# Cross-attention on one core: exponentials taken with tokens in partitions, values applied in 32x32 pieces of the array

## The chip, the cores and the metric

The kernel runs on one core of a Trainium2 chip. A core has TensorE (PE; its weight loads are shown apart as PEld), VectorE (DVE), ScalarE (ACT), GpSimd (POOL) and SyncE (SP, which issues most DMAs). The metric is device time in microseconds of one launch, as the median of several runs. Lower is better.

## The reference

One transformer block on `x` of 2 x 1024 tokens, 256 wide, with a context of 2 x 77 tokens. There are 16 heads of 16. All is float32.

```python
# layer norms inside have no gain or shift
q = (layernorm(x) @ Wq + bq); k = (ctx @ Wk + bk); v = (ctx @ Wv + bv)   # split in 16 heads of 16
att = q k^T / 4 ; att = att * mask - 1e10 * (1 - mask)
x = x + softmax(att) v @ Wo + bo
t = layernorm(x)
z = t + relu(t @ w1[0] + b1[0]) @ w2[0] + b2[0]                           # 256 -> 1024 -> 256; one expert counts
out = x + layernorm(z) * gamma + beta
```

## The kernel before

The 2048 tokens are cut into eight "halves" (`h` 0 to 7) of 256 tokens, each of them two tiles (`n` 0 and 1) of 128 tokens. Halves 0 to 3 use the first context, 4 to 7 the second.

A half goes through these steps, each a small function:

- `a_stats`, `a_norm`, `a_turn`: layer norm of `x` and four PE transposes. `a_hi` (ACT) rounds the turned input to fp32r, `a_lo` (DVE) keeps the rest, and `a_query` (L397) multiplies by `Wq` in three fp32r products: high by high, low by high, high by low. `Wq` was split in the same way at the start (`split_hi`, `split_lo`). `q_bias` (ACT) adds the bias.
- `s_scores` (L417): for each tile 8 float32 matmuls, four at a time in row strips of 32 (two heads share a strip; `kb` holds the keys with the other head's rows zeroed). Tokens lie in partitions, 16 heads x 77 keys in the free dimension.
- `s_mask` (L429, DVE) multiplies by the mask while it moves the scores from PSUM to `u` in SBUF; `s_bias` (L438, POOL) adds the large negative number; `s_max` and `s_max_act` (L443, L448, DVE) take the maximum of each head. The maximum is subtracted by DVE for 8 heads (`s_sub`, L453) and by ACT, head by head, for the other 8 (`s_sub_act`, L459).
- `s_turn` (L468): PE transposes each head, 128 tokens x 77 keys, into PSUM. `s_exp` (L473, ACT) takes the exponential of four heads at a time on the way to `pT`, which has keys in partitions.
- `s_out` (L481): values by numerators. The stationary operand is `vb`, 77 keys x 32 columns for a head (16 values and 16 ones, so that the sum of the exponentials comes out as well); 256 tokens stream. Four heads work at a time in column strips of 32.
- `s_norm` (L493 to L498, DVE): the result is turned in 32x32 blocks, and divided by the sums. `o_turn` (L511) turns back, `o_hi` and `o_lo` split, and `o_proj` (L529) multiplies by `Wo` in three fp32r products.
- `y_stats` to `y_lo`: the residual, second layer norm, transposes and split.
- FFN: `f_up` (L571) and `f_down` (L600) in three fp32r products each, with `f_relu`, `f_hi` (ACT) and `f_lo` (L589, POOL) between them; 4 steps `q` of 256 hidden units each.
- `z_stats` to `z_out`: the last layer norm and the store.

Which engine does what next is written out ahead of time: `Stages.order` takes every stage with an engine, a cost, its predecessors, the buffers (`rings`) that it needs and a rank (from `START`, `LATER`, `TILE_LAG`), and lays them one after the other; the program is then emitted in that order, and each engine keeps it. `ps` are seven PSUM banks that stages take and give back; an eighth holds small statistics. `u` has three buffers, `pT` two. 40 warm-up matmuls on zeros (`WARM`, 512 columns, L210) have the last rank and fill PE's gaps at the start.

`Wq` and `Wk` are loaded from ACT's queue, everything else from SP's, in the order of the `fetch` calls.

## Time and profile before

| | |
|---|---|
| Runs | 212.58, 211.70, 211.59 us; median 211.7 us |
| Profiled execution | 211.81 us; span from first to last instruction 210.0 us; mean granted PE clock 0.992 |
| Instructions | 1852 matmuls and 1852 weight loads on PE, DVE 336, ACT 386, POOL 151 |
| Costliest on POOL | L438 44.1 us, L589 40.9 us |
| Costliest on ACT | L473 34.2 us, L459 33.7 us, L580 26.6 us |
| Costliest on DVE | L443 and L448 25.3 us together, L429 24.1 us, L453 12.6 us, L493 11.4 us |
| DMA | 8.73 MB, of which 0.23 MB are PE's instructions |

A busy time counts the stretches in which at least one instruction of the group is under way. Matmuls are pipelined, so a mean duration is longer than the distance from one to the next. In a line of a group the last part is the time for which the engine stood idle just before, and who released it. A float32 product appears as two matmul records and two loads.

### The profile page before, as it was taken

The numbers are of one execution on the slowest core, as the hardware profiler recorded it, in microseconds if no ns is written. First come the engines' busy times: TensorE is split into PE (matmuls) and PEld (weight loads), VectorE is DVE, ScalarE is ACT, GpSimd is POOL, SyncE is SP. The second block draws the span as 40 slices with busy tenths as digits, with TensorE's granted clock in tenths as the row PEclk, the third lists the DMA queues.
The fourth block names the chain that finished last, engine by engine and source line by source line (L and its number), as shares of the span: only waits on it lengthen the run. The fifth ranks groups of instructions, "written<-read, shape, count | busy, mean of one in ns | idle before, by whom it ended". The sixth has DMA issues, their size and how long they took to land. (4 is left out here: it accounts for less than half of the span.)

```text
span 210.0 us, 4829 instructions
## 1 busy us (share of the span) xinstructions
PE 201.2 (96%) x1852; PEld 175.9 (84%) x1852; DVE 154.8 (74%) x336; ACT 155.3 (74%) x386; POOL 149.1 (71%) x151
## 2 busy tenths in 40 slices
PE   6999769999999999999999999999999999999995
PEld 1778556987996999799999778999988979999981
DVE  1678996999767992769999768999487667267234
ACT  3289998899894699993789997259997857624910
POOL 3469999899999967869998180197976573653741
PEclk9999997999999999999999999999999999999999
DMA  5997000000000000010000100001010000101011
GB/s 194 356 396 262 0 3 3 2 0 3 0 0 3 3 2 0 3 50 3 2 0 3 50 5 0 3 0 50 3 50 3 0 0 5 50 0 52 3 50 52
DMA packets 4807, 8.73 MB, mean 42 GB/s; under 512 B 662, under 2 KB 995, under 8 KB 4784
## 3 DMA queue, kind: packets, MB, share of 16 engines
q1 hardware_dynamic: 4496, 7.90, 10.3%
q10 hardware_dynamic: 288, 0.52, 0.7%
q8 instruction: 14, 0.23, 0.5%
q14 instruction: 9, 0.07, 0.1%
HBM read 6.33 MB, written 2.10 MB: 40 GB/s over the span
## 5 line engine op out<-in xcount | busy, mean ns | idle before, releaser
L438 POOL TENSOR_TENSOR u<-u,mb 128x616 f32<-128x616 f32 x32 | 44.1, 1399 | 9.5 <-DVE u L429 9.1
L589 POOL TENSOR_TENSOR hl<-h,hh 128x512 fp32r<-128x512 f32 x32 | 40.9, 1289 | 10.2 <-ACT hh L585 8.7
L571 PE MATMUL ps<-yh,w1h 128*128 128x256 f32 x128 | 37.4, 292 | 0.0
L473 ACT ACTIVATE pT<-ps 77x512 f32<-77x512 f32 x64 | 34.2, 593 | 3.9 <-PE ps L468 3.9
L600 PE MATMUL ps<-w2h,hh 128*128 128x256 f32 x128 | 37.0, 289 | 0.0
L468 PE MATMUL ps<-ident,u 128*77 128x128 f32 x256 | 34.9, 281 | 2.1 <-DVE u L453 1.3
L571 PE MATMUL ps<-yl,w1h 128*128 128x256 f32 x128 | 36.3, 283 | 0.0
L571 PE MATMUL ps<-yh,w1l 128*128 128x256 f32 x128 | 36.1, 282 | 0.0
L600 PE MATMUL ps<-w2h,hl 128*128 128x256 f32 x128 | 35.8, 279 | 0.0
L600 PE MATMUL ps<-w2l,hh 128*128 128x256 f32 x128 | 35.8, 279 | 0.0
L468 PEld LDWEIGHTS ps<-ident,u 128*77 128x77 f32 x256 | 29.5, 150 | 6.6 <-DVE u L453 2.2
L459 ACT ACTIVATE u<-u,mx 128x77 f32<-128x77 f32 x128 | 33.7, 357 | 0.6 <-DVE mx L448 0.6
L580 ACT ACTIVATE h<-ps,cols 128x256 f32<-128x256 f32 x64 | 26.6, 471 | 7.9 <-DVE ot L493 3.8
L571 PEld LDWEIGHTS ps<-yh,w1h 128*128 128x128 f32 x128 | 24.4, 191 | 1.7 <-issue 0.9
L429 DVE TENSOR_TENSOR u<-ps,mk 128x616 f32<-128x616 f32 x32 | 24.1, 792 | 2.0 <-PE ps L417 2.0
L600 PEld LDWEIGHTS ps<-w2h,hh 128*128 128x128 f32 x128 | 24.3, 190 | 1.2 <-issue 1.1
L571 PEld LDWEIGHTS ps<-yl,w1h 128*128 128x128 f32 x128 | 24.5, 191 | 0.2 <-DVE yl L554 0.2
L571 PEld LDWEIGHTS ps<-yh,w1l 128*128 128x128 f32 x128 | 24.5, 191 | 0.0
L600 PEld LDWEIGHTS ps<-w2l,hh 128*128 128x128 f32 x128 | 24.1, 188 | 0.0
L600 PEld LDWEIGHTS ps<-w2h,hl 128*128 128x128 f32 x128 | 24.1, 188 | 0.0
L585 ACT ACTIVATE hh<-h 128x512 fp32r<-128x512 f32 x32 | 20.0, 634 | 5.1 <-PE ps L600 4.5
L481 PE MATMUL ps<-pT,vb 77*32 77x256 f32 x256 | 16.8, 388 | 0.1
(96 smaller groups left out, 427.2 us busy)
## 6 DMA issues: line engine op xcount, KB each, us to landing
x<-in_x SPq DMA_DIRECT2D x8, 256.0 KB, 5.5
out<-tg SPq DMA_DIRECT2D x7, 256.0 KB, 2.0
wst<-in_L_ffn_w SPq DMA_DIRECT2D x4, 256.0 KB, 5.4
wst<-in_w SPq DMA_DIRECT2D x4, 256.0 KB, 6.0
rows<-in_rows SPq DMA_DIRECT2D x1, 512.0 KB
mk<-in_mask SPq DMA_DIRECT2D x1, 308.0 KB, 4.9
wq<-in_wq ACTq DMA_DIRECT2D x1, 256.0 KB
wk<-in_wk ACTq DMA_DIRECT2D x1, 256.0 KB, 4.6
```

The lines of the kernel that those rows point to most:

```text
L429: nc.vector.tensor_tensor(us[h, n][:, 8 * s : 8 * s + 8].rearrange("p (b h) t -> p b h t", b=2), ps[:, b0 : b0 + 2, :W].rearrange("p b (h ...
L438: nc.gpsimd.tensor_tensor(v, v, mb[:, h % HPB, n].unsqueeze(1).to_broadcast([P, 8, T]), ALU.add)
L459: nc.scalar.activation(u, u, AF.Identity, bias=mx[:, k : k + 1])
L468: nc.tensor.transpose(pt[:T, j], us[h, n][:, k], ident)
L473: nc.scalar.activation(pTs[h][:, i, :, n], pss.pop(("t", h, n, i))[:T], AF.Exp)
L481: nc.tensor.matmul(pos[h, s][r, e], lhsT=vb[:, h // HPB, k], rhs=pTs[h][:, 2 * s + e, j].rearrange("k n t -> k (n t)"), start=True, stop=True,
L571: nc.tensor.matmul(pz[:, i], lhsT=w[:, c, j * P : (j + 1) * P], rhs=v[:, c], start=(k == 0), stop=(k == 5))
L580: nc.scalar.activation(t[:, i], pz[:, i], AF.Relu, bias=b1[:, 2 * q + i : 2 * q + i + 1])
L585: nc.scalar.activation(hh[h, q], hs[h, q], AF.Copy)
L589: nc.gpsimd.tensor_tensor(hl[h, q], hs.pop((h, q)), f(hh[h, q]), ALU.subtract)
L600: nc.tensor.matmul(pys[h, ns[0]][:, n], lhsT=v[h, q][:, i, n * P : (n + 1) * P], rhs=w[:, j], start=(q == 0 and n == ns[0] and i == 0 and ...
```

## The change

Attention:

- The maximum (`s_max`) is taken by DVE for 8 heads at a time. `s_exp` is now ACT on `u` in place: one instruction for each head, `exp(u - max)` with the maximum as bias, 128 tokens in partitions and 77 keys. `s_sub`, `s_sub_act` and the PE transposes are gone.
- `s_turn` is now DVE: `u` is turned in square blocks of 32x32. One instruction turns keys 0 to 63 of all heads, a second the last 16 keys, two heads to a block. A block holds 32 keys in partitions and 32 tokens; the four row strips hold four different groups of 32 tokens.
- `s_out` works on 32x32 pieces of the array: row strip `r` holds one group of tokens and writes its own PSUM bank, column strip `j` one head. For a half it is 4 groups of heads x 3 pieces of keys (0 to 31, 32 to 63, the last 16) x 4 x 4 = 192 float32 calls of 64 columns. It takes four banks at once. `vb` holds the values in all four row strips and three pieces (`v_proj`, `v_copy`, `v_ones`, `ctz`); the value bias goes through `Wo` into `bo` once (`o_rows`, `o_bias`).
- `s_norm` turns with two instructions instead of one.
- The query and output projections are plain float32: four calls for a half each instead of 12 fp32r ones. `a_lo`, `o_hi`, `o_lo` and the splits of `Wq` and `Wo` go.

Beside it: all loads are on SP's queue, with small vectors packed behind the mask; some small copies go from DVE to ACT; 200 warm-up matmuls of 256 columns instead of 40 of 512; in the last half two `f_lo` are on DVE, the residual enters the FFN's sum by a matmul with the identity (`f_first`), and the centring (`z_center`) is done beside POOL's power. Costs, ranks and lags of the order are new throughout.

```diff
-WARM = 40
+WARM = 200
...
-GAP = 0.44
-TILE_LAG = 11.6
+GAP = 0.3
+TILE_LAG = 36.1
...
     def a_query(h):
...
             for d in range(2):
-                for w, v in ((wqh, xh[h]), (wqh, xl[h]), (wql, xh[h])):
-                    nc.tensor.matmul(
-                        pq[:, c], lhsT=w[:, d, c * P : (c + 1) * P], rhs=v[:, d], start=(k == 0), stop=(k == 5)
-                    )
-                    k += 1
+                nc.tensor.matmul(
+                    pq[:, c], lhsT=wq[:, d, c * P : (c + 1) * P], rhs=xh[h][:, d], start=(d == 0), stop=(d == 1)
+                )
...
-    def s_turn(h, n, i):
-        pt = pss["t", h, n, i] = bank(("tr", h, n, i), (P, 4, P))
-        for j, k in enumerate(heads(i)):
-            nc.tensor.transpose(pt[:T, j], us[h, n][:, k], ident)
...
+    def s_max(h, n, s):
+        mx = mxs[h, n, s] = work([P, 8], "mx", f"mx{h}_{n}{s}", 12)
+        nc.vector.tensor_reduce(mx, us[h, n][:, 8 * s : 8 * s + 8], AX.X, ALU.max, negate=True)
+
+    def s_exp(h, n, s, i):
+        mx = mxs[h, n, s] if i == 0 else mxs.pop((h, n, s))
+        for k in range(4 * i, 4 * i + 4):
+            u = us[h, n][:, 8 * s + k]
+            nc.scalar.activation(u, u, AF.Exp, bias=mx[:, k : k + 1])
+
+    def s_turn(h, n):
+        if n == 0:
+            pTs[h] = work([P, 40, 2, 32], "pT", f"pT{h}", RINGS["pT"])
+        u = us.pop((h, n))
+        nc.vector.transpose(pTs[h][:, :32, n], u[:, :, :64])
+        nc.vector.transpose(pTs[h][:, 32:, n], u[:, :, T - 16 :])
+
+    def s_out(h):
+        pos[h] = got = st.all["po", h]["slots"]["ps"]
+        for g in range(4):
+            s, e = g // 2, g % 2
+            for k in range(3):
+                for r in range(4):
+                    for j in range(4):
+                        i = 8 * s + 2 * j + e
+                        v = slice(32 * r, 32 * r + 32)
+                        o = ps[32 * j : 32 * j + 32, got[r], 128 * s : 128 * s + 128]
+                        nc.tensor.matmul(
+                            o.rearrange("p (n e t) -> p n e t", n=2, e=2)[:, :, e],
+                            lhsT=vb[v, h // HPB, k, i],
+                            rhs=pTs[h][v, 2 * i + k if k < 2 else 32 + i // 2],
+                            start=(k == 0), stop=(k == 2), skip_group_check=True,
+                            tile_position=(32 * r, 32 * j),
+                        )
...
     def s_norm(h, s):
+        t = work([P, 2, 4, 2, 32], "ot", f"ot{h}_{s}", 1)
+        for z in range(2):
+            b0 = pos[h][2 * z]
+            nc.vector.transpose(
+                t[:, :, 2 * z : 2 * z + 2].rearrange("p n r e d -> p n r (e d)"),
+                ps[:, b0 : b0 + 2, 128 * s : 128 * s + 128].rearrange("p r (n c) -> p n r c", n=2),
+            )
...
+    def f_first(h, n):
+        pys[h, n] = bank(("dt", h, n), (P, 2, E))
+        nc.tensor.matmul(pys[h, n][:, n], lhsT=ident, rhs=tg[h][:, n], start=True, stop=False, skip_group_check=True)
...
-    fetch("wqd", 0.9, lambda: None, ring=stage_ring("hh", "wqh", "wql"))
...
+    fetch_x(0, 1.3)
+    fetch("cd", 0.45, load, c_sb, a["c"])
+    fetch("wkd", 0.75, load_matrix, "wk", "wk", "hl", ring=stage_ring("hl", "pk"))
+    fetch("mkd", 0.9, load, mkc, a["mask"])
+    fetch("wqd", 0.7, load, wq, a["wq"])
+    fetch_x(1)
```

## The prediction

> **What bounds the kernel now.** I read the busy shares first, then the table by stage, then the groups of instructions, then PE's timeline. The chain that ended last covers the final 4 us only and says nothing of the middle.

> ```profile
> PE 201.2 (96%) x1852; PEld 175.9 (84%) x1852; DVE 154.8 (74%) x336; ACT 155.3 (74%) x386; POOL 149.1 (71%) x151
> ```

> ```profile
> 26.00:60.00 34.00, 32.03 (x306) 27.69 (x305) 29.64 (x62) 31.68 (x83) 31.88 (x35) 0.95 0.01 2
> 60.00:100.00 40.00, 39.73 (x402) 35.80 (x401) 29.93 (x64) 31.36 (x81) 33.76 (x32) 1.00 0.02 8
> 100.00:140.00 40.00, 39.90 (x401) 35.45 (x401) 34.49 (x70) 30.71 (x81) 24.22 (x21) 1.00 0.02 8
> 140.00:180.00 40.00, 39.69 (x382) 36.36 (x381) 28.67 (x60) 32.58 (x81) 28.26 (x24) 1.00 0.05 19
> 180.00:204.00 24.00, 24.00 (x203) 23.60 (x203) 11.14 (x32) 11.24 (x23) 12.34 (x12) 1.00 0.07 26
> ```

> The columns are the stage, its length, and the busy time of PE, PEld, DVE, ACT and POOL. From 60 to 204 us PE stands still for 0.7 us in all, while the other three are busy 78, 79 and 72% of 60 to 180, and under half of the last stage, where only FFN is left. So PE's queue sets the time, and what leaves it is gained, as long as no other engine takes its place. In 26 to 60 the others are at 87 to 94% and PE already loses 6%.

> ```profile
> L473 ACT ACTIVATE pT<-ps 77x512 f32<-77x512 f32 x64 | 34.2, 593 | 3.9 <-PE ps L468 3.9
> L468 PE MATMUL ps<-ident,u 128*77 128x128 f32 x256 | 34.9, 281 | 2.1 <-DVE u L453 1.3
> L459 ACT ACTIVATE u<-u,mx 128x77 f32<-128x77 f32 x128 | 33.7, 357 | 0.6 <-DVE mx L448 0.6
> L481 PE MATMUL ps<-pT,vb 77*32 77x256 f32 x256 | 16.8, 388 | 0.1
> L453 DVE TENSOR_TENSOR u<-u,ps 128x616 f32<-128x616 f32 x16 | 12.6, 789 | 0.2
> L493 DVE STREAM_TRANSPOSE ot<-ps 128x512 f32<-128x512 f32 x16 | 11.4, 713 | 6.5 <-PE ps L481 2.6 <-ACT qs L405 2.0 <-ACT u L459 1.6
> ```

> These are the groups that the change rebuilds. A matmul's mean holds its latency, so I price PE by distances between starts, from its timeline:

> ```profile
> 64.24 0.66 PE L468 MATMUL ps<-ident,u 128*77 128x128 f32 x4 [0.17 <-ACT qs L405]
> 64.83 0.81 PE L417 MATMUL ps<-kb,qs 32*128 32x154 f32 x16
> 65.57 1.07 PE L481 MATMUL ps<-pT,vb 77*32 77x256 f32 x16
> 66.57 0.81 PE L417 MATMUL ps<-kb,qs 32*128 32x154 f32 x16
> 67.31 0.38 PE L600 MATMUL ps<-w2h,hh 128*128 128x256 f32 x1
> ...
> 100.61 0.41 PE L417 MATMUL ps<-kb,qs 32*128 32x154 f32 x4
> ```

> A float32 product is two load-and-matmul pairs: 128 calls of `s_out` are 256 records. Four pairs in four strips of the array start together (0.41 us for four, at most 0.39 for one); in the trace 6 to 7 ns apart, 6.7 ns on average. Sixteen such pairs of L481 hold PE for 1.0 us (65.57 to 66.57), strip changes included: four rounds of 0.216 us and some 0.2 us for the change of strips.

> **The change on PE.**
> - The transposes of L468 go: 256 starts, 0.109 us apart in the trace, 27.9 us. All of it lay in the packed queue: -27.9.
> - The old `s_out` goes: 16 x 1.0 = -16.0.
> - The new `s_out` comes: 4 groups x 3 key pieces x 4 x 4 = 192 calls, 384 pairs, 768 instructions for a half of 256 tokens. The work in a piece is small: 64 columns against 256 of L481, so a round takes 0.216 x 64 / 256 = 0.054 us, and 24 rounds of 16 pairs 1.3 us. The starts take more: 384 x 6.7 ns = 2.57 us, and 0.2 for the strips. I take 8 x 2.77 = +22.2, because start distance is the nearest row; 8 x 1.5 = 12.0 is the low end.
> - The two projections: 192 fp32r matmuls 0.118 us apart (L397, L529: 22.7) become 64 calls in float32. The nearest row is L308, whole array, 256 columns, halves 0.21 us apart, so 64 x 0.43 = 27.5: +4.8.

> PE together: -27.9 - 16.0 + 22.2 + 4.8 = -16.9.

> **How fast PE gets its instructions** is the term that no row shows, since before never issues 768 tiny ones in a row. Two rows bound it. The densest stretch above, 64.83 to 67.31, is 96 instructions in 2.48 us, 26 ns each, and there the array was the limit; at that pace 768 take 19.8 us. The other row is the fetching of PE's code:

> ```profile
> q8 instruction: 14, 0.23, 0.5%
> ```

> 14 fetches for 3704 loads and matmuls, so some 256 instructions each, and 0.5% of 16 engines' 210 us is 1.2 us a fetch. Three fetches back to back are 3.6 us for a half; if execution (2.57) and fetching take turns, 6.2. I take 2.57, since the first fetches can run ahead while PE works on FFN matmuls, and keep 6.2 for the range: 8 x 3.6 = +29.

> [...]

> **The other engines.** They must not grow, and by rows they do not.
> - ACT loses L459 (33.7), L473 (34.2), `o_hi` (4.7) and two splits (1.2). It gains 256 exponentials with a bias per head, priced as L459: 33.7 / 128 = 0.263 each, 67.4; and some 4 for copies that DVE did. Net about -2.
> - DVE loses L453 (12.6), `a_lo` and `o_lo` (5.5 each) and 3.3 of small ones. It gains 16 pairs of square-block transposes, 1280 elements each. DVE's rows give 0.69 us for 512 elements and 0.42 for 256, so 1.04 ns an element and 0.16 fixed: 1.65 us, of which neighbours overlap some 0.08 each, so 1.5 to 1.65, 24 to 26.4. `s_norm`'s split transposes add 16 x 0.16 = 2.6, two `f_lo` 1.4. Net +1 to +4.
> - POOL loses a split (1.3) and two `f_lo` (2.6).

> So DVE 156 to 159, ACT 153, POOL 145, in a span some 15 us shorter: some 83% of the main part instead of 77%. PE's loss was 0.6% at 77% and 5.8% at 92%; in between, 2.7% of 165 us is 4.4, against 2.65 lost in 26 to 180 before: +2.

> **Beginning and end.** `wq` and `wk` move from ACT's queue to SP's, behind `x0` and `c`, with `wk` ahead of the mask and `wq` after it; `x1` waits behind all of these. The splits of `wq` (a wait of 2.1 on its DMA, then ACT 0.6 and DVE 0.7) are gone. I cost it at nothing, since PE does keys and warm-ups until 15.5 us; -1 or +1.5 if that cover fails. The 200 warm-up matmuls fill planned gaps up to 61 us, half the width of those in before; one in front of ready work delays it by 0.11 us, so I give them +1 (0 to +3). In the last half two `f_lo` move from POOL (1.29) to DVE (0.69), the residual joins the sum by a matmul ahead of time (a 0.43 us DVE add goes) and one 0.49 us pass is done beside POOL's power. Only part was on the path: -1.

> Sum on the span: 210.0 - 16.9 + 2 + 1 - 1 = 195.1. The profiled execution took 211.81 for 210.0, so 196.9; the median of the runs is 0.1 lower: **196.8 us**.

> **Rivals.**
> - *Instructions come too slowly (slower than before).* Place: the 768 instructions of `s_out`, behind which everything in PE's queue waits. The other terms save 27.9 + 16.0 - 4.8 - 2 = 37.1, so with 0.2 for strips the break-even is 37.1 / 8 - 0.2 = 4.4 us per half, 5.8 ns an instruction. At 10 ns: 8 x 7.9 - 37.1 = +26, 238 us. At 26 ns: 8 x 20.2 - 37.1 = +124, 336 us. For it: no row shows a sustained pace under 26 ns, and fetches of 1.2 us add up to 3.6 or 6.2 us. Against it: starts 6.7 ns apart per pair, and PE showed no gap at its 14 fetches. Chance 0.24.
> - *The fetch is the pace, but overlaps:* 3.6 us per half, 8 x 1.03 = +8: about 205 us. Chance 0.12.
> - *The bound moves.* ACT, DVE and POOL, each about 150, are chained by the masked scores (`u`, three buffers, now held until the turning). If they only keep the 78% of 60 to 180, DVE's 157 take 201 and the first 8 us, where it has little to do, make 209, and 211 with what lies around the span: no gain. The 87 to 94% of 26 to 60 speak against it. Chance 0.06.
> - *The pieces do not run 16 at a time* but four, as L417 and L481 do: 96 rounds of 0.054, 5.2 us per half, 8 x 2.6 = +21: 218 us. It is part of the first rival's 0.24.

> **The numbers.** The forecast has 0.58: starts at 1.3 to 3 us per half. The range goes from 183 (the low end of `s_out`, -10, no loss by crowding, -2, a sooner start, -1) to 229 (the 6.2 us of alternate fetching, +29, and warm-ups at +3); what lies outside is mainly the first rival at 9 ns an instruction or more. The forecast's own range is 183 to 204 (warm-ups and start at their worse ends, `s_out` at 3 us). A measurement of this kernel can tell about 0.5% from no change. Faster: 0.70; same: 0.04; slower: 0.26.

> **What would show it.** Right: L468's group gone; the new `s_out` holding PE 2.5 to 3 us for a half, its starts 6 to 7 ns apart; some 35 fetches on PE's code queue without gaps of PE beside them; DVE's two transposes of the turning near 1.2 and 0.4 us; PE, DVE and ACT all at 80% or more. Wrong: "issue" as PE's releaser at `s_out`, spans of 5 us and more for a half, or PE waiting for DVE's turning.

## The result, and the profile after

The changed kernel took 267.47 us (median of 4 runs, 265.93 to 268.74) where the kernel before took 211.69: a ratio of 1.262, with a 95% interval of 1.2545 to 1.2695. The forecast was 196.8 us, its range ended at 229. The first rival, that instructions come too slowly, had the right place and the right sign, and too low a price.

The profiled execution spans 265.5 us. From its page, the busy shares, TensorE's granted clock in 40 slices, and the queue that brings the engines' code:

```profile
PE 229.2 (86%) x4636; PEld 205.1 (77%) x4636; DVE 155.2 (58%) x346; ACT 156.8 (59%) x452; POOL 145.5 (55%) x151
PEclk9999975995699689959999599599996896899999
q8 instruction: 36, 0.59, 0.9%
```

DVE, ACT and POOL do what they did before (154.8, 155.3, 149.1), in 55 us more. PE is busier by 28 us and yet at 86% instead of 96%. The clock drops to half in eight stretches, 61.4 us in all; before, in one of 3.4 us and at the very end. `q8` is taken for the queue of PE's code, since its fetches rise with PE's loads and matmuls: 14 for 3704 before, now 36 for 9272, one for every 258; each moves 16384 bytes.

The groups that the change built (line, engine, tiles, shape, count; busy us, mean ns; idle before it and what ended that):

```profile
L467 ACT ACTIVATE u<-u,mx 128x77 f32<-128x77 f32 x256 | 67.2, 350 | 0.4 <-DVE mx L461 0.3
L489 PE MATMUL ps<-pT,vb 32*32 32x64 f32 x3072 | 38.3, 246 | 27.9 <-issue 26.7
L489 PEld LDWEIGHTS ps<-pT,vb 32*32 32x32 f32 x3072 | 33.5, 111 | 32.0 <-issue 29.1
L475 DVE STREAM_TRANSPOSE pT<-u 128x1024 f32<-128x1024 f32 x16 | 19.7, 1232 | 2.1 <-ACT u L467 2.1
L476 DVE STREAM_TRANSPOSE pT<-u 128x256 f32<-128x256 f32 x16 | 6.4, 401 | 0.0
```

The exponentials cost 67.2 us (forecast 67.4) and DVE's turning 26.1 (24 to 26.4). What is out of line is L489, the new `s_out`: its loads stand 29.1 us for "issue", which means that the profile shows nothing they wait for. The list of waits has it again, with the number of times and the longest, and with who is behind it:

```profile
DVE ot L504 <- PE ps L489: 45.9, 8, 7.5
POOL hl L592 <- ACT hh L587: 44.9, 13, 10.1
ACT h L582 <- PE ps L573: 36.5, 13, 7.4
PEld ps L489 <- issue: 29.1, 14, 2.8
PE ps L489 <- issue: 26.7, 13, 2.6
```

And this is one half on the timeline of PE's loads (start, length, instructions in the group, idle before):

```profile
56.90 1.80 PEld L489 LDWEIGHTS ps<-pT,vb 32*32 32x32 f32 x177 [0.17 <-DVE pT L476]
61.07 1.71 PEld L489 LDWEIGHTS ps<-pT,vb 32*32 32x32 f32 x128 [2.37 <-issue]
64.52 1.14 PEld L489 LDWEIGHTS ps<-pT,vb 32*32 32x32 f32 x79 [1.74 <-issue]
```

Between the standstills lie exactly 128 loads with their 128 matmuls, 256 instructions. They run in 1.7 us or less, and the next 128 begin 3.45 us after the first did (64.52 - 61.07); in two other halves it is 3.73. From first to last load the eight halves take 8.1, 8.6, 8.7, 8.4, 5.8, 8.3, 8.5 and 6.8 us, 63.2 in all, and 30.4 of these are 13 standstills of 1.9 to 2.9 us from load to load, two for five halves and one for three. (The first half has 1.5 us more near its start, and the profile names DVE's mask product, L448, as what ended that wait.)

The trace's record of single transfers shows what ends a standstill. In each of the 13, a transfer of 16384 bytes on PE's code queue ends, and PE's next load starts 1.23 to 1.42 us after that end. Where a half has two standstills, the transfer for the second begins 1.1 us after the first one ended, and takes 0.9 to 1.4 us. So the 3.45 us have three parts: 1.1 from the beginning of a block to the beginning of the next one's transfer, about 1.0 of transfer, and 1.3 until the block is used.

Around them the stages:

```profile
26.00:60.00 34.00, 27.39 (x728) 21.85 (x726) 28.04 (x54) 25.02 (x90) 28.42 (x29) 0.85 0.01 3
60.00:100.00 40.00, 33.17 (x774) 29.69 (x775) 20.76 (x46) 22.41 (x68) 21.46 (x27) 0.79 0.01 3
140.00:180.00 40.00, 31.64 (x903) 29.92 (x899) 21.90 (x49) 17.23 (x48) 14.90 (x14) 0.83 0.05 16
```

(Stage, length, busy time of PE, PEld, DVE, ACT, POOL, granted clock, DMA share, GB/s.) No engine is full, and the clock falls to 0.79 and 0.83.

An account of where PE's queue spent its time, by the distance from the start of one matmul to the start of the next (a wait counts for the matmul that it follows):

| us | before | forecast | after |
|---|---|---|---|
| `s_out` | 16.1 | 22.2 | 68.2 |
| transposes of `u` (L468) | 31.2 | 0 | 0 |
| FFN, up and down | 94.4 | 94.4 | 104.9 |
| warm-ups | 14.6 | 15.6 | 26.0 |
| two projections | 24.4 | 29.2 | 31.4 |
| `v_proj` | 1.5 | not priced | 5.8 |

`s_out` is 46 us over its term. FFN matmuls, untouched, start 10.5 us later in sum, since part of them run at half clock: 98 of the 768 start 0.213 us apart instead of 0.118.

A word on the comparisons below: times of one kernel differ by up to 7 us (e15_both: 203.36 at a granted clock of 0.992, 210.13 at 0.967), so ratios are taken over runs that were not disturbed, and where a run has no ratio its median is given with that caution.

### The profile page after: what moved, and what is told of

Read it like the earlier page. It is cut to its first block, busy times and chain, and to the rows that moved or that the text cites. A ratio compares the mean times of both kernels' runs of the same rounds, so it can differ in the third digit from the quotient of the medians.

```text
span 265.5 us, 10423 instructions
## 1 busy us (share of the span) xinstructions
PE 229.2 (86%) x4636; PEld 205.1 (77%) x4636; DVE 155.2 (58%) x346; ACT 156.8 (59%) x452; POOL 145.5 (55%) x151
## 4 chain that ended last, share of the span: by engine, by line
PE 72%; issue 12%; POOL 7%; DMA 4%; DVE 3%; SPq 1%; ACT 1%; POOLq 0%
PE ps L573 20%; PE ps L603 19%; PE ps L489 14%; PE ps L531 5%; PE ps L210 4%; PE ps L417 4%; POOL u L457 4%; PE ps L436 3%; DMA rows<-in_rows 2%; PE ps L547 2%; DMA wv<-in_wv 2%; DVE u L448 1%; POOL w1l L271 1%; POOL x L410 1%; SPq L225 1%
## 5 line engine op out<-in xcount | busy, mean ns | idle before, releaser
L467 ACT ACTIVATE u<-u,mx 128x77 f32<-128x77 f32 x256 | 67.2, 350 | 0.4 <-DVE mx L461 0.3
L489 PE MATMUL ps<-pT,vb 32*32 32x64 f32 x3072 | 38.3, 246 | 27.9 <-issue 26.7
L489 PEld LDWEIGHTS ps<-pT,vb 32*32 32x32 f32 x3072 | 33.5, 111 | 32.0 <-issue 29.1
L582 ACT ACTIVATE h<-ps,mkc 128x256 f32<-128x256 f32 x64 | 26.5, 467 | 38.7 <-PE ps L573 36.5
L573 PE MATMUL ps<-yh,w1h 128*128 128x256 f32 x128 | 41.0, 320 | 2.5 <-issue 2.5
L504 DVE STREAM_TRANSPOSE ot<-ps 128x256 f32<-128x256 f32 x32 | 12.5, 429 | 46.0 <-PE ps L489 45.9
L573 PEld LDWEIGHTS ps<-yh,w1h 128*128 128x128 f32 x128 | 27.8, 217 | 3.3 <-issue 3.2
L448 DVE TENSOR_TENSOR u<-ps,mkc 128x616 f32<-128x616 f32 x32 | 24.1, 790 | 8.9 <-PE ps L436 8.9
L210 PE MATMUL ps<-zero 128*128 128x256 bf16 x200 | 25.9, 287 | 2.8 <-DVE u L448 1.1
L461 DVE TENSOR_REDUCE mx<-u 128x8 f32<-128x616 f32 x32 | 23.9, 778 | 2.7 <-POOL u L457 2.7
L210 PEld LDWEIGHTS <-zero 128*128 128x128 bf16 x200 | 20.1, 103 | 6.8 <-issue 2.7
```

Source lines behind the costliest of these rows:

```text
L210: nc.tensor.matmul(bank(("wm", i))[:, :256], lhsT=zero[:, :P], rhs=zero, start=True, stop=True)
L448: nc.vector.tensor_tensor(us[h, n][:, 8 * s : 8 * s + 8].rearrange("p (b h) t -> p b h t", b=2), ps[:, b0 : b0 + 2, :W].rearrange("p b (h ...
L461: nc.vector.tensor_reduce(mx, us[h, n][:, 8 * s : 8 * s + 8], AX.X, ALU.max, negate=True)
L467: nc.scalar.activation(u, u, AF.Exp, bias=mx[:, k : k + 1])
L489: nc.tensor.matmul(o.rearrange("p (n e t) -> p n e t", n=2, e=2)[:, :, e], lhsT=vb[v, h // HPB, k, i], rhs=pTs[h][v, 2 * i + k if k < 2 el ...
L504: nc.vector.transpose(t[:, :, 2 * z : 2 * z + 2].rearrange("p n r e d -> p n r (e d)"), ps[:, b0 : b0 + 2, 128 * s : 128 * s + 128].rearra ...
```

## The experiments

Three theories at first. A: PE's code comes in blocks of 256 instructions, only one block is ahead, and the next takes longer to come than tiny matmuls take to use one up. B: the pieces get in each other's way in the array or in PSUM. C: the sequencer needs some 10 ns for each instruction, evenly.

**e1_thin: all instructions, a fraction of the data.**

```diff
-            for k in range(3):
+            for k in (2, 0, 1):
...
+                        w = 32 if k == 2 else 2
...
-                            o.rearrange("p (n e t) -> p n e t", n=2, e=2)[:, :, e],
+                            o.rearrange("p (n e t) -> p n e t", n=2, e=2)[:, :, e, :w],
```

> The changed kernel, with two of the three key pieces of s_out streaming 4 columns instead of 64 (60 of 64 columns of these pieces are left out; the piece with the last 16 keys is whole). Instructions stay as they are, the array's work in s_out falls to 38%. Theory A (PE's code comes in blocks of 256 instructions, the next block is asked for too late, and each border inside s_out costs some 2.3 us): nothing changes, some 14 gaps of 2 to 3 us inside s_out, 8 us from the first to the last load of a half, 262 to 270 us. Theory B (the pieces are in each other's way in the array or in PSUM): s_out falls below 4 us a half, under 235 us. Theory C (a sequencer that issues slowly, evenly, at some 10 ns an instruction): time unchanged, but no gaps at borders.

Measured 267.71 us, ratio 1.2624 (1.2537 to 1.271). The halves take 7.8, 8.7, 8.2, 8.1, 6.4, 8.3, 8.8 and 6.9 us. Its waits:

```profile
PE ps L490 <- issue: 31.9, 15, 3.2
PEld ps L490 <- issue: 31.7, 16, 3.3
```

A sixteenth of the columns in two thirds of the pieces changes nothing (267.71 us for 267.47): what is streamed does not matter here, and B falls.

**e2_onekey: a third of the instructions.**

```diff
-            for k in range(3):
+            for k in (2,):
```

> The changed kernel with only the last of the three key pieces in s_out: 64 calls, 256 instructions for a half instead of 768; keys 0 to 60 are left out of the sums. Theory A: at most one border inside a half, so 1.6 us of running and up to 2.4 of standing, 4 us instead of 8; 36 fetches become 20; with less half clock 215 to 232 us. Theory B: a third of 8 us, 2.7, no gap that lies on a border of 256 instructions. Theory C: 2.7 us, no gaps.

Measured 203.17 us, ratio 0.9615 (0.9584 to 0.9646). Seven of eight halves take 1.21 us for 256 instructions, 4.7 ns each, without a gap; no wait for "issue" is left at this line, and PE is at 95%:

```profile
PE 191.6 (95%) x2588; PEld 169.5 (84%) x2588; DVE 154.3 (77%) x346; ACT 155.3 (77%) x452; POOL 145.5 (72%) x151
```

C falls: PE can start an instruction every 4.7 ns for 256 of them. A had expected up to 2.4 us of standing in each half and 215 to 232 us; that no border stood still here would fit a next block that is fetched while PE works on the long matmuls ahead of the burst. (In the changed kernel there is such a case: one transfer runs from 138.0 to 138.9 us, the burst begins at 139.62, and its first 256 pairs run without a gap.) But with `s_out` nearly free, the prediction's sum would give 195.1 - 22.2 + 8 x 1.2 = 183 for this span, and it is 201.3. Something else is missing, too; e8 and e13 to e17 are about that.

**e4_bf16: half of the instructions, all keys.** The numerators leave the exponential in bfloat16 (and the values are kept in it), so a call is one pair of instructions.

```diff
-    vb = const([P, B, 3, H, 2 * D], "vb")
+    vb = const([P, B, 3, H, 2 * D], "vb", mybir.dt.bfloat16)
...
-            nc.scalar.activation(u, u, AF.Exp, bias=mx[:, k : k + 1])
+            nc.scalar.activation(es[h, n][:, 8 * s + k], us[h, n][:, 8 * s + k], AF.Exp, bias=mx[:, k : k + 1])
...
-            pTs[h] = work([P, 40, 2, 32], "pT", f"pT{h}", RINGS["pT"])
+            pTs[h] = work([P, 40, 2, 32], "pT", f"pT{h}", RINGS["pT"], mybir.dt.bfloat16)
```

> The changed kernel with numerators and values in bf16 instead of float32: one load and one matmul for a call instead of two of each, so 384 instructions for a half and 24 fetches, and a quarter of the array's work. Theory A: 1.5 borders a half, so some 2.3 us of running and 3.5 of standing, 5 to 6 us a half; DVE's turning at best as before; 215 to 242 us. Theory B: 2 us a half and under 210 us. Theory C: 3.9 us a half without gaps, some 225 us.

Measured 210.70 us, ratio 0.9879 (0.9836 to 0.9923). Five halves take 1.55 to 1.58 us. Two take 2.1 and 4.0, with a standstill inside, and the first 3.1, of which 1.5 are the wait near its start. A had expected 5 to 6 us for every half and 215 to 242 us: as in e2_onekey, most borders passed. The array's work falls here too (in the kernel before, a bf16 matmul of 512 columns, L210, and each half of a float32 call of 256, L308, are both 0.216 us from start to start), so by itself this run does not tell A from B; e1_thin does.

```profile
PEld L491 <- issue: 4.9, 6, 2.4
PE ps L491 <- issue: 2.7, 2, 2.3
```

**e5_flood: the suspect put into the kernel before.** Behind the last matmul of each half's `s_out`:

```diff
+        if s == 1:
+            for k in range(192):
+                j = k % 4
+                nc.tensor.matmul(
+                    ps[32 * j : 32 * j + 32, BANKS, 256:257],
+                    lhsT=ident[:32, :32],
+                    rhs=ident[:32, :1],
...
```

> The kernel before, with 192 float32 calls of one column added behind the second s_out of each half (768 instructions, four column strips in turn, into a free corner of PSUM that nobody reads; nothing waits for them but PE's queue). There is next to no array work. Theory A: three borders a half at 2.3 us and 768 x 6 ns of running, so 8 to 11 us a half, 64 to 90 us in all and more by half clock: 280 to 310 us. Theory B: 384 starts at 6.7 ns, 2.6 us a half: 232 us. Theory C at 10 ns: 7.7 us a half without gaps, 273 us.

Measured 295.15 us, ratio 1.3979 (1.393 to 1.4028): 83.8 us for 6144 instructions that compute next to nothing. The same standstills, 128 pairs apart:

```profile
PEld ps L492 <- issue: 34.6, 21, 2.6
PE ps L492 <- issue: 31.9, 18, 2.5
```

**e9_flood256 and e10_flood512: the price by the block.** The same with 64 calls (256 instructions) and 128 calls (512).

```diff
-            for k in range(192):
+            for k in range(64):
```

> The kernel before with 64 one-column float32 calls (256 instructions, one block) behind the second part of s_out of each half. Theory A: the next block was asked for when its predecessor was begun, during FFN work, and is there; 256 instructions run in about 1.6 us and the border behind them is met at FFN pace, so a gap is rare: 8 x 1.6 to 2.4 = 13 to 19 us, 224 to 231 us. A price per instruction (83.8 us of e5_flood for 8 x 768, 13.6 ns each) would give 8 x 256 x 13.6 ns = 28, 239 us.

> As e9_flood256 with 128 calls, 512 instructions, two blocks. Theory A: one or two borders per half stand still for up to 2.5 us: 8 x (3.1 + 2.3 to 4) = 43 to 57, 254 to 268 us. A price per instruction: 8 x 512 x 13.6 ns = 56, 267 us. What tells them apart is the step from 256 to 512 against the step from none to 256: at least twice as large under A, equal otherwise.

Measured 222.15 us, ratio 1.0497 (1.0428 to 1.0566), and 269.14 us, ratio 1.2734 (1.2684 to 1.2784). So none, 256, 512 and 768 instructions are 211.2, 222.2, 269.1 and 295.2 us: steps of 11, 47 and 26. The first block is nearly paid at its run time (six of eight halves take 1.05 us, 4.1 ns an instruction, with no gap); the second brings the standstills:

```profile
PEld ps L492 <- issue: 2.3, 3, 1.2
PE ps L492 <- issue: 1.7, 2, 1.1
```

```profile
PEld ps L492 <- issue: 20.6, 12, 2.6
PE ps L492 <- issue: 19.0, 10, 2.5
```

(First 256, then 512.) In one half of e5_flood, standstills end at 169.61 and at 173.06 us:

```profile
169.61 1.15 PEld L492 LDWEIGHTS ps<-ident 32*32 32x32 f32 x128 [1.62 <-issue]
173.06 1.80 PEld L492 LDWEIGHTS ps<-ident 32*32 32x32 f32 x128 [2.30 <-issue]
```

That is 3.45 us again, though the block between ran in 1.05 us from first to last load and the one in the changed kernel in 1.6. So the pace is the block's, and a shorter run only makes a longer gap. The first step is smaller than a price per instruction would make it (28), the second much larger: A. (Both times lie 1 to 2 us outside A's ranges.) The 512's 57.9 us exceed run time and standstills (some 43); of the rest 8 are longer FFN work (L583 and L612 together, from 94.4 to 102.5 us; five of the 40 slices of the clock line show 5 tenths); what the others are was not followed up.

**e6_spread and e6_fine: the standstill undone, all instructions kept.** `s_out` is cut into three (six) parts of 128 (64) pairs, and between two parts PE gets FFN matmuls of other halves for about 1.45 us.

```diff
-    def s_out(h):
+    def s_out(h, part):
...
-        for g in range(4):
+        for gk in range(4 * part, 4 * part + 4):
+            g, k = gk // 3, gk % 3
```

> The changed kernel with the same 768 loads and matmuls of s_out per half, in three parts of 128 pairs, with one FFN stage of 12 matmuls (about 1.5 us on TensorE) or more put between two parts; the rest of the order as it was. Theory A (a block of 256 instructions is there about 3.45 us after its predecessor was begun; faster consumption stands still): a part takes 1.56 us and the FFN stage about 1.6, 3.2 us per 280 instructions, so what is left of a gap is 0.2 to 0.6 us per border; the gaps of s_out fall from 31.8 us to under 10, and the time to 230 to 250 us (some of the gain may come back as waits, since the four banks are held longer). Theory C (each instruction costs 10 ns, evenly) and theory B (the pieces get in each other's way): the parts take 2.7 us or more each as before, time 262 to 272 us.

> As e6_spread, in six parts of 64 pairs with an FFN stage between any two. Theory A: 0.78 + 1.6 us per 152 instructions, 4.0 us per 256, more than the 3.45 us that a block takes to come: no gaps within s_out except where the order has no FFN work left for it; time 225 to 245 us. Theories B and C: 262 to 272 us, 0.78 us per 64 pairs is not reached.

Measured 259.82 us, ratio 1.2312 (1.2242 to 1.2381), and 290.37, ratio 1.3732 (1.3646 to 1.3818). The mechanism behaved as A says; the times were missed. In e6_spread ten of 24 parts of 128 pairs run in 1.21 us, without a gap, and the waits for "issue" fall from 29.1 to 9.0 us; in e6_fine 42 of 48 parts of 64 pairs run in 0.61 us or less. These are all instructions with all of their data at 4.7 ns each, which neither B nor C allows:

```profile
PEld ps L490 <- issue: 9.0, 15, 2.1
PE ps L490 <- issue: 5.8, 10, 1.9
```

What it cost instead shows elsewhere: the output projection's column in PE's account goes from 13.3 to 17.7 us and that of the scores from 12.5 to 18.5. In e6_fine the same cost is larger (24.9 and 20.8) and outweighs the gain. The likely reason, not shown by a run of its own, is that four of seven banks are held while other work goes between, in an order that was not made for it.

**e7_warm and e8_bf16w: the warm-ups.** Four of five of the 200 warm-up calls are left out, in the changed kernel and in e4_bf16.

```diff
-            st.all[key]["fn"]()
+            if key[0] != "wm" or key[1] % 5 == 0:
+                st.all[key]["fn"]()
```

> The changed kernel with only every fifth of its 200 warm-up calls (40, as many as the kernel before has), everything else in the same order. The gaps of s_out stay (31.8 us). If the warm-ups stand in TensorE's way (26 us from start to start after, 14.6 before): 257 to 264 us. Rival: they fill idle time and keep the clock up, 267 us or up to 5 us more, with more half-clock stretches than 54.6 us.

> The changed kernel with numerators and values in bfloat16 (384 instructions of s_out per half, as e4_bf16, 210.7 us) and every fifth warm-up call only. Warm-ups on TensorE's path: 200 to 207 us, granted clock as in e4_bf16 (0.975). Rival, that they lie in idle time: 209 to 213 us.

Measured 265.07 us, ratio 1.2542 (1.2471 to 1.2614), not to be told from the changed kernel's; and 211.57, ratio 1.0021 (0.9989 to 1.0053), somewhat slower than e4_bf16, at a profiled clock of 0.935 instead of 0.975. The warm-ups lie in idle time, and in both runs the clock went down without them (e7_warm: 0.851, the changed kernel 0.884). That they stood in PE's way was wrong.

**e11_proj: the float32 projections alone,** in the kernel before, with the order of everything else kept.

```diff
-                for w, v in ((wqh, xh[h]), (wqh, xl[h]), (wql, xh[h])):
...
+                nc.tensor.matmul(
+                    pq[:, c], lhsT=wq[:, d, c * P : (c + 1) * P], rhs=xh[h][:, d], start=(d == 0), stop=(d == 1)
+                )
```

> The kernel before with the two projections in float32 alone (64 calls for 192, no splits of the operands), everything else in the same order. The prediction's term: TensorE +4.8 us; DVE loses 11 and ACT 5 us, which were not the bound: 211.4 + 4.8 = 216, between 213 and 218 us. If float32 calls cost more than 0.43 us each here (31.4 us from start to start in the changed kernel for 24.4 before, +7): 218 to 220 us. If the removed splits were on the path: 209 to 213 us.

Measured 214.87 us, ratio 1.0171 (1.0114 to 1.0227): +3.7 where the term was +4.8. The two projections take 27.8 us from start to start (forecast 27.5).

**e12_order: another order for e4_bf16,** with half of the warm-ups and other ranks.

> A version meant to beat both: e4_bf16 with half of the warm-up calls and with ranks of its own in place of those of the changed kernel (so another order of the same work). If e4_bf16 (210.7 us) is limited by the order and the filling of the first 80 us: 203 to 208 us. Rival, that ACT, DVE and POOL are the limit whatever the order: 209 to 213 us.

Measured 218.86 us: a miss. Its waits at the pieces are 10.1 us where e4_bf16 has 2.7, and its halves of `s_out` take 25.6 us from first to last load where e4_bf16's take 17.0:

```profile
PE ps L491 <- issue: 10.1, 5, 2.4
```

The number of instructions is nearly the same; which borders fall into `s_out`, and what runs ahead of them, is decided by the order.

**e13 to e17: where the rest of the gain went.** PE's work without warm-ups is 190.1 us before and 171.0 in e4_bf16, 19 less, but the span is only 3.3 shorter. In 26 to 60 us that work fell from 32.0 to 22.6 us, and the transposes had 9.9 us there before:

```profile
26.00:60.00 34.00, 9.87 (x70) 8.43 (x69) 0.95 0.01 2
```

(Kernel before, L468 alone: PE, PEld, clock.) So in this stretch the work left and no time with it. Which engine holds it was asked by relieving them, all in e4_bf16 and in its order: ACT (e13_wide: one exponential and one maximum for four heads, which holds as long as no head's maximum lies far below another's), POOL (e14_pool: the bias on 8 of 77 keys only), both (e15_both), DVE (e16_dve: the maximum over 8 of 77 keys only), all three (e17_three).

```diff
-            nc.scalar.activation(es[h, n][:, 8 * s + k], us[h, n][:, 8 * s + k], AF.Exp, bias=mx[:, k : k + 1])
+        v = slice(8 * s + 4 * i, 8 * s + 4 * i + 4)
+        nc.scalar.activation(es[h, n][:, v], us[h, n][:, v], AF.Exp, bias=mx[:, i : i + 1])
...
-        v = us[h, n][:, 8 * s : 8 * s + 8]
-        nc.gpsimd.tensor_tensor(v, v, mb[:, h % HPB, n].unsqueeze(1).to_broadcast([P, 8, T]), ALU.add)
+        v = us[h, n][:, 8 * s : 8 * s + 8, T - 8 :]
+        nc.gpsimd.tensor_tensor(v, v, mb[:, h % HPB, n, T - 8 :].unsqueeze(1).to_broadcast([P, 8, 8]), ALU.add)
...
-        nc.vector.tensor_reduce(mx, us[h, n][:, 8 * s : 8 * s + 8], AX.X, ALU.max, negate=True)
+        nc.vector.tensor_reduce(mx, us[h, n][:, 8 * s : 8 * s + 8, T - 8 :], AX.X, ALU.max, negate=True)
```

> e4_bf16 with one exponential for four heads (64 of 128x308 for 256 of 128x77) and one maximum for the four, everything else in the same order: ACT loses some 40 of 67 us. If the chain of exponentials sets the filling of 26 to 60 us, where TensorE's work other than warm-ups fell from 32.0 us (before) to 22.6 (e4_bf16): that work rises by 4 us or more there and the time falls from 210.7 to 200 to 206 us. Rival, that DVE (32.3 of 34 us busy) and POOL (32.2) hold that stretch as well: 208 to 211 us.

> e4_bf16 with POOL's mask bias on 8 of 77 keys only (leaves out 69 keys of the bias): POOL loses some 35 of 44 us, ACT and DVE keep theirs. If ACT alone sets the filling: 209 to 211 us. If POOL's passes stand in the chain of the fill as well: 204 to 208 us.

> Both edits (leaves out 69 keys of the bias). If the three other engines together hold 26 to 60 us, only this one frees it: TensorE's work there back to 28 us or more and 197 to 203 us. Rival, that the order of TensorE's queue or the end holds the time: above 206 us.

> e4_bf16 with the maximum taken over 8 of 77 keys (leaves out 69 keys of it): DVE, busy 32 to 33 of the 34 us of 26 to 60 in e4_bf16, e13_wide and e14_pool alike, loses some 20 of 155 us. If DVE holds that stretch: TensorE's work there without warm-ups rises from 22.6 to 26 us or more, and the time falls to 202 to 207 us. If the order of the queues holds it: 209 to 211 us.

> e16_dve with the wide exponentials and the short bias as well (leaves out 69 keys of the maximum and of the bias): all three engines relieved by 20 to 40 us each. If their work holds 26 to 60 us, the time goes to 195 to 202 us. If it is the order (what TensorE, in order, has to wait for and what stands behind it): above 204 us.

Measured: e13_wide 209.84 us, ratio 0.9844 (0.981 to 0.9878); e14_pool 209.09, ratio 0.9815 (0.9762 to 0.9867); e15_both 208.04 (median of 203.36 to 210.13); e16_dve 209.9, ratio 0.9911 (0.987 to 0.9953); e17_three 208.88 (203.97 to 210.85). The stretch in e4_bf16, e13_wide and e17_three, columns as above:

```profile
26.00:60.00 34.00, 30.28 (x599) 24.79 (x597) 32.26 (x65) 29.47 (x104) 32.15 (x39) 0.90 0.01 3
```

```profile
26.00:60.00 34.00, 29.75 (x604) 24.77 (x604) 32.93 (x64) 19.79 (x42) 32.64 (x40) 0.95 0.01 3
```

```profile
26.00:60.00 34.00, 30.97 (x613) 25.70 (x612) 26.12 (x62) 18.53 (x40) 22.07 (x38) 0.90 0.01 3
```

PE's 30 us hold 7 to 9 of warm-ups. The chain of waits through these 34 us goes 31.5% through ACT's exponentials in e4_bf16; in e13_wide, where they are short, POOL's bias takes over with 28%; with both short, DVE's maximum, mask product and turning have 49%; with all three short, PE's own warm-ups and DVE's products stand there:

```profile
28.25 3.76 PE ps L210 x33
...
42.97 1.51 DVE u L448 x2
44.48 0.13 DVE mx L462
44.61 1.15 DVE pT L478
...
50.62 0.55 PE ps L550 x3
```

No single engine was the holder: three are nearly equally full, and with all three relieved PE still has only 24 us of work there, where it had 32. That it takes its queue in the given order and stands at the next half's scores would explain this, but no run shows it. The ratios give a gain of 1 to 2%, far from the 10 us at stake. Only the quickest runs of e15_both (203.36) and e17_three (203.97) come nearer, 5 us below the quickest of e4_bf16 (208.52); the profiles above are not of these runs. What an order made for these costs would give is open; the one attempt, e12_order, ran into the borders of the code.

By their ratios e13_wide and e4_bf16 are 1.6 and 1.2% below the kernel before, by the medians of all runs 0.7 and 0.3%, and far below the changed kernel. They are the quickest versions here that leave no key out, with numerators in bfloat16 and, for e13_wide, under the condition above.

## Why the prediction was wrong

**The step that failed** is one sentence: "I take 2.57, since the first fetches can run ahead while PE works on FFN matmuls". In the five halves with two standstills, the second block's transfer began only 1.1 us after the block before it was begun, so no more than one block was ahead. `s_out` uses three, and had one or two standstills in each half. Measured, each further 256 instructions take 3.45 us or a little more, so that 768 cost one block at run time (1.2 to 1.6 us) and two at 3.45, 8.1 to 8.5 us, and not 2.77; six halves took 8.1 to 8.7, two whose borders fall well 5.8 and 6.8. Eight halves, with the waits around them: 68.2 us, +46 on a term of 22.2.

**The upper bound of that term was too low as well.** 6.2 us took fetch and execution in turns with 1.2 us for a fetch, the share of the engines that the transfer occupies. In the trace the transfer is about 1.0 us long, but it begins 1.1 us after the block before was begun and is used 1.3 us after its end, so it is less than a third of the 3.45. The row of the profile gives the occupation and not the delay, and I took the one for the other.

**The first rival** named the place and put the break-even at 5.8 ns an instruction. Measured over a half, 63.2 / 8 / 768 is 10.3 ns, and at 10 ns the rival's sum was 238 us. Most of the other 29 us are in the account above: FFN +10.5, idle time that the warm-ups fill +10, `v_proj` +4, projections +2. Its mechanism, a slow even pace, was not the one: between the standstills the pieces run at 4.7 to 4.8 ns an instruction at full clock and 6.0 to 6.4 in the half-clock stretches.

**L468, -27.9, "all of it lay in the packed queue".** The transposes went, but PE was busy with them for 9.9 us in 26 to 60, where the prediction's own table had the other engines at 87 to 94% and PE already losing 6%. The row was there and I did not split the term by stage. That the saving was lost there is shown (32.0 us of work fell to 22.6 in the same 34 us); what held the stretch stays open. With it goes the +2 for crowding, which was for the main part alone.

**Right, or nearly:** exponentials 67.2 (67.4), turning 26.1 (24 to 26.4), projections +3.7 alone (+4.8), the pieces 16 at a time (e6_spread: 128 pairs in 1.21 us, 3.6 for a half; 96 rounds of four would have been 5.2), and the warm-ups, whose +1 I doubted after the result and which e7_warm and e8_bf16w found off the path. **Left out of the sum:** `v_proj`, 64 calls instead of 4 (5.8 us for 1.5), and any price for the clock. **What would show it wrong** had been written down rightly: "issue" as PE's releaser at `s_out`, 5 us and more for a half.

## What to carry to other kernels

Count instructions per stage, not only columns: here a burst on PE could use one block of 256 instructions at its own pace (six of eight halves of e9_flood256), but beyond that it needed 3.45 us for the next 256, 13.5 ns for each. So small tiles were quick where the whole burst stayed near one block (e2_onekey: 1.21 us in seven of eight halves); long matmuls between the borders took most of the standstills away (29.1 to 9.0 us in e6_spread), but left the time at 259.82 us. A price that no row shows should get an upper bound from the worst way in which its parts can chain, not from the occupation of one part. And a saving on the engine that bounds the kernel has to be split by stage: where the others were as full, what left the queue left a hole (in 26 to 60 us PE's work fell from 32.0 to 22.6 us, and the span by 3.3).
